# A state-space convolution, two rounds of adapters and a feed-forward layer: moving the convolution's tables, its adds, its input loads and its stores

## The chip, the core and the metric

The kernel runs on one core of a Trainium2 chip. The metric is the device time of one execution, in microseconds (us). The kernel before took 2495.6 us (median of three runs, 2495.14 to 2496.21). The profiled execution took 2497.51 us, of which the span of the core's instructions is 2495.7 us.

## The reference

`x` has 32 sequences of 64 rows of 1024 numbers (`B`, `H`, `L`), float32. Four layers follow each other, each added to `x`:

```python
x = x + conv(x)      # row h is convolved with its own kernel K[h], causal, plus D[h] * x; masked at a length
x = x + x @ w1[id1]  # one 1024 x 1024 matrix for each sequence, picked from 16
x = x + x @ w2[id2]  # the same with other matrices and ids
x = x + down(silu(gate(x)) * up(x))   # 1024 -> 2752 -> 1024, each product with a low-rank term picked by id3
```

The convolution's kernel is a sum over 64 complex exponentials: `K[h, l] = 2 * Re(sum_n Ct[h, n] * exp(dtA[h, n] * l))`. It is computed on the chip as a product of two tables, with `l = 32 a + b`: one table in `a` (tile `gt`), one in `b` (tile `et`), each made of a sine and an exponential, and a small matmul for each row h that sums over n.

## The kernel before, in words

**Layout.** The 32 sequences are four chunks of 8 (`NCK`, `BC`). A chunk of `x` is a tile of 128 partitions by 8 x 512 numbers, 16 KB a partition, 2 MB in all (`x_tile`). Chunks 0 and 1 lie in `xpool` (two buffers). Chunks 2 and 3 lie in `x2pool` only while the convolution runs; then they are stored to DRAM (tiles `xd`, L141, on ScalarE's DMA queue), which frees their space for the feed-forward's pools, and each is loaded back when its chunk is near (`between`, `parked`).

**Convolution** (`convolution`, from L560). First some sixty small VectorE operations on 128 x 64 and 128 x 128 tiles (L617 to L686), from the tables `par` (L576) and `cst` (L105). Then the 64 rows go in four groups of 16 (`HG`). `kernels(g)` makes a group's tables: four products `bth` and `brho` (`powers`), three sines (`sine`, L597 to L605: seven VectorE operations and one ScalarE activation each), five more products, all on 128 x 512 tiles; 16 matmuls into `pk` (L745); a copy to `ks` (L753), an add (line 591 is the helper `tt` of all these products), and a store to DRAM (`kp`, L757 and L758, ScalarE's queue). `convolve(g)` reads the stored kernel back from SP's queue as Toeplitz blocks `hk` of 1 MB for two rows (L770, three buffers) together with `uf`, 0.5 MB for four rows (L765), runs 32 matmuls for each `hk` (L781) into `pc`, multiplies by the mask into `tmp` (two buffers), and for every four rows adds `tmp` to the four chunks of `x` (four adds of 128 x 256). All products and adds are VectorE's. In the program `kernels(g + 1)` stands ahead of `convolve(g)`, so that TensorE, which keeps the program's order, meets the `pk` matmuls of group 1 ahead of the first `pc`. The four loads of `x` (L692) are on ScalarE's queue.

**Adapters** (`adapter`, `adapters`). Chunk c needs, for 8 sequences and 2 layers, 8 weight blocks of 0.5 MB each: 128 loads, 64 MB. They go through `wpool` (nine buffers of 4 KB a partition) on SP's queue (L176), and each pair of blocks feeds four matmuls (L182). A pair of sequences ends with two ScalarE copies to `y` (L192), eight transposes (L200) and two VectorE adds to `x` (L204).

**Feed-forward** (`ffn`). For each of 11 strips of the hidden dimension `gated` loads four weight blocks, combines them on VectorE (`stationary`, L347 to L350), runs seven products for gate and for up (L377), copies and adds the results (`u` L391, `c` L393 and on), and adds the low-rank term `lt` (L329). The down product is in `po` (L505), four parts `h` for each of two blocks. The low-rank columns come from `columns`: eight small loads on ScalarE's queue into `raw`, then a ScalarE copy to `at` (L255). `prepare(c)` makes the low-rank products of gate and up of a chunk (`pl_g`, `pl_u`, L276) and the combinations `xd` of its `x`; for a later chunk it stands in the last part `h` of the chunk before.

**Order.** While chunk c is in its feed-forward, the adapters of chunk c + 1 run between its strips: `other(share)` counts work and takes the next of 17 pieces when it is due. For chunk 0 there is nothing to run beside: its adapters run alone, all of them ahead of its feed-forward. TensorE's order is the program's; the other engines' orders are set by a scheduler at build time. [...]

Of the kernel before, what the change touches and what calls it, by code (L numbers as in the profile page):

```python
# [8 lines left out]
F32 = mybir.dt.float32  # L9
# [18 lines left out]
MB = 6  # L28
SEG = 3
# [6 lines left out]
HG = 16  # L36
# [25 lines left out]
def kernel(  # L62
# [42 lines left out]
    nc.sync.dma_start(cst, consts)  # L105
    ident = cst[:, CO_ID : CO_ID + P]
    bmask = cst[:, CO_BM : CO_BM + 2 * H]

# [22 lines left out]
    def x_tile(pool, c, tag):  # L131
        return pool.tile([P, KT, TC], F32, tag=tag, name=f"x{c}")

    xs = [x_tile(xpool, c, "x") for c in range(2)]
    parked = []
    with tc.tile_pool(name="x2pool", bufs=1) as x2pool:
        late = [x_tile(x2pool, c, f"x{c}") for c in range(2, NCK)]
        convolution(tc, cst, xt, xf, ssm, lens, xs + late, ps_tile)
        for c, x_c in enumerate(late, 2):
            d = dpool.tile([P, KT, TC], F32, tag=f"xd{c}", name=f"xd{c}")  # L140
            nc.scalar.dma_start(d, x_c)  # L141
            parked.append(d)

    loads = []
    ypool = ctx.enter_context(tc.tile_pool(name="ypool", bufs=2))

    def adapter(w, layer, b0, pending):
        c, lo = b0 // BC, (b0 % BC) * H
        es = []
        for b in (b0, b0 + 1):
            with ExitStack() as after:
                if len(loads) > 1:

                    after.enter_context(tc.issue_after(loads[-2]))
                es.append(
                    nc.values_load(  # L160
                        ids_sb[0:1, layer * B + b : layer * B + b + 1],
                        engines=[SP],
                        min_val=0,
                        max_val=NE - 1,
                    )
                )
        acc = [acc_tile(f"pa{layer}_{b0}_{i}") for i in range(2)]
        for kt in range(KT):
            if kt == KH:
                yield  # L170
            if kt == (c == 0) and pending:
                residual(*pending.pop())
            wts = []
            for s, e in enumerate(es):
                wt = wpool.tile([P, L], F32, tag="w", name=f"wa{layer}_{b0 + s}_{kt}")
                load = nc.sync.dma_start(  # L176
                    wt, w[bass.ds(e, 1), kt].rearrange("e p f -> p (e f)")
                )
                wts.append(wt)
            for i in range(2):  # L180
                for s in range(2):
                    nc.tensor.matmul(  # L182
                        acc[i][s * H : (s + 1) * H, :],
                        xs[c][:, kt, lo + s * H : lo + (s + 1) * H],
                        wts[s][:, i * 512 : (i + 1) * 512],
                        start=(kt == 0),
                        stop=(kt == KT - 1),
                    )
        loads.append(load.ins)
        y = ypool.tile([P, L], F32, tag="y", name=f"y{layer}_{b0}")  # L190
        for i in range(2):
            nc.scalar.copy(y[:, i * 512 : (i + 1) * 512], acc[i])  # L192
        pending.append((c, lo, y, f"{layer}_{b0}"))
        yield
# [24 lines left out]
    hpool = ctx.enter_context(tc.tile_pool(name="hpool", bufs=1))  # L219
    gpool = ctx.enter_context(tc.tile_pool(name="gpool", bufs=2))  # L220
    apool = ctx.enter_context(tc.tile_pool(name="apool", bufs=MB))

# [194 lines left out]
    def prepare(c):  # L417

        x_c = xs[c]
        for name, table in (("g", ag), ("u", au)):  # L420
            at = columns(table, c, KT, f"{name}_{c}")
            ps = low_rank(at, KT, lambda i: (x_c[:, i, :], P), f"{name}_{c}")
            nc.vector.tensor_mul(tms[name], ps, bmask)
# [12 lines left out]
    def ffn(c, xb, others):  # L436
# [6 lines left out]
        def other(share, of=2 * FM * AT_GATED + (2 * KH - 2) * AT_DOWN):  # L443
            due[0] += share * (NPIECE + 1)
            while due[1] * of < due[0]:
                next(others, None)
                due[1] += 1
# [8 lines left out]
        for block, (m0, m1) in enumerate(BLOCKS):  # L456
# [26 lines left out]
            for h in range(KH):  # L483
                name = f"{c}_{block}_{h}"
                if last and h == KH - 1 and c + 1 < NCK:
                    for _ in others:
                        pass
                    ready = prepare(c + 1)
# [56 lines left out]
                if not last or h < KH - 2:  # L545
                    other(AT_DOWN)
        return ready

    with tc.manual_schedule(engines={PE}):
        for _ in adapters(0):  # L550
            pass
        xb = prepare(0)
        for c in range(NCK):
            xb = ffn(c, xb, adapters(c + 1) if c + 1 < NCK else iter(()))


def convolution(tc, cst, xt, xf, ssm, lens, xs, ps_tile):
# [9 lines left out]
    with ExitStack() as ctx:  # L567
# [8 lines left out]
        nc.sync.dma_start(par, ssm)  # L576
        ln = s1.tile([P, B], I32, tag="len", name="ln")
        nc.sync.dma_start(ln, lens.partition_broadcast(P))
        aim, cre, cim, dskip = (par[:, i, :] for i in range(2, 6))
# [10 lines left out]
        def tt(o, a, b, op):  # L590
            nc.vector.tensor_tensor(o, a, b, op)
            return o
# [98 lines left out]
        for c in range(NCK):  # L691
            nc.scalar.dma_start(xs[c], xt[:, c])  # L692

# [3 lines left out]
        def kernels(g):  # L697

            h0 = g * HG
            shape = [P, HG, LQ]  # L700

            def over_l(ap):
                return ap[:, h0 : h0 + HG].unsqueeze(2).to_broadcast(shape)

# [5 lines left out]
            def big(tag):  # L710
                n[0] += 1
                return s1.tile(shape, F32, tag=f"b{tag}", name=f"b{tag}{g}_{n[0]}")

            def powers(at, tag):
                theta, rho = big(f"th{tag}"), big(f"rho{tag}")
                tt(theta, over_l(y), over_h(at), ALU.mult)
                tt(rho, over_l(x), over_h(at), ALU.mult)
# [17 lines left out]
            gt = s2.tile(shape, F32, tag="gt", name=f"gt{g}")  # L735
            et = s2.tile(shape, F32, tag="et", name=f"et{g}")
# [7 lines left out]
            for i in range(HG):  # L744
# [7 lines left out]
            ks = s2.tile([LQ, HG, LQ], F32, tag="ks", name=f"ks{g}")  # L752
            nc.vector.tensor_copy(ks.rearrange("a h b -> a (h b)"), ps[:LQ, : HG * LQ])  # L753
            k0 = ks[0:1, :, 0]
            tt(k0, k0, dskip[0:1, h0 : h0 + HG], ALU.add)
            kp = dram.tile([HG, KROW], F32, tag=f"kp{g}", name=f"kp{g}")
            nc.scalar.dma_start(kp[:, :P], zero)  # L757
# [3 lines left out]
        def convolve(g, kp):  # L761
            for h0 in range(0, HG, 4):
                ha = g * HG + h0
                uf = s3.tile([P, 4, KT, B], F32, tag="uf", name=f"uf{ha}")
                nc.sync.dma_start(uf, xf[:, ha : ha + 4])  # L765
                tmp = s2.tile([P, 4, KT * B], F32, tag="tmp", name=f"tmp{ha}")
                for i in range(0, 4, 2):
                    hk = s3.tile([P, 2, L], F32, tag="hk", name=f"hk{ha + i}")

                    nc.sync.dma_start(  # L770
                        hk,
                        bass.AP(
                            tensor=kp.tensor,
                            offset=kp[h0 + i : h0 + i + 1, 1:2].offset,
                            ap=[[1, P], [KROW, 2], [1, L]],
                        ),
                    )
                    ps = ps_tile(f"pc{ha + i}").rearrange("p (i t) -> p i t", i=2)
                    for j in range(2):
                        for d in range(KT):  # L780
                            nc.tensor.matmul(  # L781
                                ps[:, j, d * B :],
                                hk[:, j, d * P : (d + 1) * P],
                                uf[:, i + j, : KT - d, :].rearrange("p k b -> p (k b)"),
                                start=(d == 0),
                                stop=(d == KT - 1),
                            )
                    tt(
                        tmp[:, i : i + 2, :],
                        ps,  # L790
                        maskf.unsqueeze(1).to_broadcast([P, 2, KT * B]),
                        ALU.mult,
                    )
                tv = tmp.rearrange("p i (k b) -> p k b i", b=B)
                for c in range(NCK):
                    xv = xs[c].rearrange("p k (b h) -> p k b h", h=H)[
                        :, :, :, ha : ha + 4
                    ]
                    tt(xv, xv, tv[:, :, c * BC : (c + 1) * BC, :], ALU.add)

        ready = kernels(0)
        for g in range(H // HG):
            nxt = kernels(g + 1) if g + 1 < H // HG else None
            convolve(g, ready)
            ready = nxt

# [132 lines left out]
```

## Time and profile before

| | us |
|---|---|
| median of three runs | 2495.6 |
| profiled execution | 2497.51 |
| its span | 2495.7 |
| TensorE busy in the span | 2397.1 (96%) |
| VectorE busy | 1141.7 (46%) |
| ScalarE busy | 337.7 (14%) |
| GpSimd busy | 50.1 (2%) |
| DMA moved | 500.53 MB, mean 201 GB/s |

A matmul's end is modelled in these records, so a busy TensorE is not one at its peak: while it waits for weights that arrive one by one its matmuls show as long ones. In the lines below "PE" is TensorE's matmuls, "PEld" its weight loads, DVE VectorE, ACT ScalarE, POOL GpSimd, "SPq" and "ACTq" the queues of SP and ScalarE. A group's line gives the source line, the engine, the operation, out<-in, shapes, the count; then busy time, the mean of one in ns, and the idle time just before with what ended it.

### The profile page before, as it was taken

How to read it: one execution, taken by the hardware profiler on the slowest of the kernel's cores; microseconds unless marked ns; L12 is line 12 of the kernel's file. 1: busy time of each engine (PE TensorE's matmuls, PEld its weight loads, DVE VectorE, ACT ScalarE, POOL GpSimd, SP SyncE). 2: the span in 40 equal slices, each digit the busy share in tenths (PEclk: the TensorE clock that was granted, in tenths of full speed). 3: DMA queues.
4: the chain of work that ended last, by engine and by line, in shares of the span. 5: the costliest groups of instructions: out<-in, count | busy, mean ns of one | idle time of the engine just before them, and what ended most of it. 6: DMA issues, size and time to landing. Idle time of an engine off the chain costs nothing.

```text
span 2495.7 us, 34972 instructions
## 1 busy us (share of the span) xinstructions
PE 2397.1 (96%) x13600; PEld 1802.8 (72%) x13600; DVE 1141.7 (46%) x2184; ACT 337.7 (14%) x644; POOL 50.1 (2%) x52
## 2 busy tenths in 40 slices
PE   0998898999999999999999999999999999999999
PEld 0995234777777777768686776777777688888887
DVE  8732002445344553444344453444345445554554
ACT  3100001111011111111011201111011101210110
POOL 0000000000000000000000000000000000000000
PEclk9999999999999999999999999999999999999999
DMA  7787997555655546565656547564746544223221
GB/s 294 245 281 280 378 409 279 220 202 198 211 207 203 211 144 239 202 225 182 222 186 226 191 158 243 193 244 156 246 164 248 182 135 136 85 74 107 89 66 62
DMA packets 176167, 500.53 MB, mean 201 GB/s; under 512 B 19778, under 2 KB 69250, under 8 KB 174978
## 3 DMA queue, kind: packets, MB, share of 16 engines
q1 hardware_dynamic: 145762, 453.43, 51.4%
q10 hardware_dynamic: 26144, 31.24, 3.6%
q0 software_dynamic: 4096, 13.63, 1.6%
q8 instruction: 107, 1.75, 0.3%
q14 instruction: 58, 0.48, 0.1%
HBM read 485.36 MB, written 12.88 MB: 200 GB/s over the span
## 4 chain that ended last, share of the span: by engine, by line
PE 89%; DMA 8%; DVE 2%; ACTq 1%; issue 1%; ACT 0%; SPq 0%; DVEq 0%
PE pf L377 42%; PE po L505 21%; PE pa L182 15%; PE pc L781 6%; DMA wa<-in_w 6%; PE pe L319 2%; PE py L200 1%; PE pl_d L276 1%; PE po L302 1%; DMA x<-xd 1%; DMA out_y<-x 0%; DMA x<-in_xt 0%; PE pl_g L276 0%; ACTq L250 0%; ACTq L244 0%
## 5 line engine op out<-in xcount | busy, mean ns | idle before, releaser
L377 PE MATMUL pf<-xd,wf 128*128 128x256 f32 (+1 forms) x2816 | 668.6, 382 | 0.0
L377 PEld LDWEIGHTS pf<-xd,wf 128*128 128x128 f32 (+1 forms) x2816 | 524.0, 188 | 96.8 <-issue 9.7
L182 PE MATMUL pa<-wa,x 128*64 128x512 f32 x2048 | 495.1, 603 | 26.4 <-DMA wa<-in_w 20.2
L377 PE MATMUL pf<-xd,s 128*128 128x256 f32 (+1 forms) x2112 | 500.9, 380 | 5.0 <-ACT c L393 4.9
L377 PEld LDWEIGHTS pf<-xd,s 128*128 128x128 f32 (+1 forms) x2112 | 397.0, 188 | 65.8 <-ACT c L393 5.3
L182 PEld LDWEIGHTS pa<-wa,x 128*64 128x64 f32 x2048 | 150.1, 137 | 336.1 <-issue 251.9
L505 PE MATMUL po<-act,wd 128*128 128x256 f32 x704 | 177.0, 385 | 0.0
L505 PE MATMUL po<-actd,s 128*128 128x256 f32 x704 | 172.9, 379 | 0.0
L505 PE MATMUL po<-actd,wd 128*128 128x256 f32 x704 | 172.9, 379 | 0.0
L402 DVE TENSOR_TENSOR c<-pf,u 128x256 f32<-128x256 f32 (+1 forms) x88 | 37.3, 424 | 267.8 <-PE pf L377 267.8
L505 PEld LDWEIGHTS po<-act,wd 128*128 128x128 f32 x704 | 130.3, 190 | 33.3 <-issue 11.0
L781 PE MATMUL pc<-uf,hk 128*128 128x256 f32 (+7 forms) x1024 | 149.8, 310 | 0.0
L781 PEld LDWEIGHTS pc<-uf,hk 128*128 128x128 f32 x1024 | 146.0, 193 | 3.6
L505 PEld LDWEIGHTS po<-actd,s 128*128 128x128 f32 x704 | 133.6, 190 | 18.4
L505 PEld LDWEIGHTS po<-actd,wd 128*128 128x128 f32 x704 | 133.6, 190 | 18.4
L329 ACT COPY lt<-pe 128x512 f32<-128x512 f32 (+1 forms) x176 | 90.3, 599 | 260.7 <-PE pe L319 146.8
L347 DVE TENSOR_TENSOR s<-wf 128x512 f32<-128x512 f32 x88 | 60.7, 690 | 131.8 <-PE po L505 50.8
L204 DVE TENSOR_TENSOR x<-py,x 128x512 f32<-128x512 f32 x64 | 42.9, 687 | 153.9 <-PE py L200 153.7
L406 DVE TENSOR_TENSOR c<-c,lt 128x1024 f32<-128x1024 f32 (+1 forms) x88 | 107.5, 1222 | 5.1 <-DVE c L404 0.5
L192 ACT COPY y<-pa 128x512 f32<-128x512 f32 x64 | 37.5, 585 | 467.3 <-PE pa L182 442.8
L347 DVE TENSOR_TENSOR s<-wd 128x384 f32<-128x384 f32 x64 | 33.4, 522 | 138.4 <-PE po L505 79.7
L400 ACT COPY c<-pf 128x256 f32<-128x256 f32 (+1 forms) x88 | 32.7, 372 | 418.9 <-PE pf L377 418.9
(146 smaller groups left out, 1611.5 us busy)
## 6 DMA issues: line engine op xcount, KB each, us to landing
wa<-in_w SPq DMA_DIRECT2D x512, 512.0 KB
wf<-in_wg SPq DMA_DIRECT2D x88, 512.0 KB
wf<-in_wu SPq DMA_DIRECT2D x88, 512.0 KB
wd<-in_wd SPq DMA_DIRECT2D x96, 384.0 KB
hk<-kp SPq DMA_DIRECT2D x32, 1024.0 KB
x<-in_xt ACTq DMA_DIRECT2D x4, 2048.0 KB
uf<-in_xf SPq DMA_DIRECT2D x16, 512.0 KB
wd<-in_wd SPq DMA_DIRECT2D x32, 256.0 KB
```

What stands on the lines that cost most here:

```text
L182: nc.tensor.matmul(acc[i][s * H : (s + 1) * H, :], xs[c][:, kt, lo + s * H : lo + (s + 1) * H], wts[s][:, i * 512 : (i + 1) * 512], start= ...
L192: nc.scalar.copy(y[:, i * 512 : (i + 1) * 512], acc[i])
L204: nc.vector.tensor_add(cols, ps, cols)
L319: nc.tensor.matmul(ps[:n, at_ : at_ + 2 * H], bt[pair(j), g, i, :n], tms["gu"[g]][pair(j)], start=(g + i == 0), stop=True, skip_group_chec ...
L329: nc.scalar.copy(lt[:n, :, 2 * H * j : 2 * H * (j + 1)], ps[:n].rearrange("p (i t) -> p i t", i=4),)
L347: nc.vector.tensor_add(s1, a21, a22)
L377: nc.tensor.matmul(ps, ws[j][:, kt, :n], xb[j][:, kt, :], start=start and kt == 0, stop=kt == KH - 1, skip_group_check=True,)
L400: nc.scalar.copy(cq[:n, 0], pa)
L402: nc.vector.tensor_add(cq[:n, 1], pb, u[:n])
L406: nc.vector.tensor_add(cf, cf, lt[:n, g].rearrange("p i t -> p (i t)"))
L505: nc.tensor.matmul(pss[j], ws[j][:k, i, :], ab[m - m0][j], start=(m == m0 and home[j] % 2 == 0), stop=(m == m1 - 1), skip_group_check=True,)
L781: nc.tensor.matmul(ps[:, j, d * B :], hk[:, j, d * P : (d + 1) * P], uf[:, i + j, : KT - d, :].rearrange("p k b -> p (k b)"), start=(d == ...
```

## The change

Four things are changed in the convolution, and with them where its data lies.

- **Groups.** Five groups of 8, 8, 16, 16 and 16 rows in place of four of 16. `kernels(g + 1)` now stands inside group g, behind its first four rows where g has 8, behind its first eight where it has 16; the first `pc` comes straight behind the first `pk`.
- **Engines.** `bth` and `brho` and the adds to `x` go from VectorE to GpSimd. The copy of `pk` to `ks` goes from VectorE to ScalarE.
- **Loads.** `par`, `cst` and `lens` are the first DMAs on SP's queue, the four chunks of `x` follow on the same queue, then `uf` and `hk`. The ids (`ids`, `il`) come behind the first of the `hk`. The first adapter's first eight weight loads are put behind the sixth `hk`: four of them go to new buffers (`epool`), which with `wpool`'s nine makes thirteen.
- **Chunks 2 and 3.** They and the four new buffers lie on the other side of the SBUF. Their stores (`park`) are issued behind the last ScalarE copy of chunk 0's adapters, no longer at the convolution's end; the pool `apool` takes their place.

Beside these, `prepare` is split: the gate's part stands one part `h` earlier than the up's, the adapters' pieces of the next chunk are due one part earlier, and several pools wait for tiles rather than for the whole of an earlier pool.

```diff
+EARLY = 4
-HG = 16
+GROUPS = (8, 8, 16, 16, 16)
+HG = max(GROUPS)
...
-    nc.sync.dma_start(cst, consts)
...
+    right = ExitStack()
+    x2pool = right.enter_context(tc.tile_pool(name="x2pool", bufs=1, side="right"))
+    epool = right.enter_context(tc.tile_pool(name="epool", bufs=1, side="right"))
+    late = [x_tile(x2pool, c, f"x{c}") for c in range(2, NCK)]
+    early = [epool.tile([P, L], F32, tag=f"e{i}", name=f"early{i}") for i in range(EARLY)]
+    blocks = convolution(tc, cst, consts, xt, xf, ssm, lens, xs + late, ps_tile)
+    parked = []
+
+    def park():
+        for c, x_c in enumerate(late, 2):
+            d = dpool.tile([P, KT, TC], F32, tag=f"xd{c}", name=f"xd{c}")
+            nc.scalar.dma_start(d, x_c)
+            parked.append(d)
...
-    with tc.tile_pool(name="x2pool", bufs=1) as x2pool:
-        late = [x_tile(x2pool, c, f"x{c}") for c in range(2, NCK)]
-        convolution(tc, cst, xt, xf, ssm, lens, xs + late, ps_tile)
-        for c, x_c in enumerate(late, 2):
-            d = dpool.tile([P, KT, TC], F32, tag=f"xd{c}", name=f"xd{c}")
-            nc.scalar.dma_start(d, x_c)
-            parked.append(d)
...
-                wt = wpool.tile([P, L], F32, tag="w", name=f"wa{layer}_{b0 + s}_{kt}")
+                name = f"wa{layer}_{b0 + s}_{kt}"
+                wt = early.pop(0) if early else wpool.tile([P, L], F32, tag="w", name=name)
...
-        def other(share, of=2 * FM * AT_GATED + (2 * KH - 2) * AT_DOWN):
+        def other(share, of=2 * FM * AT_GATED + (2 * KH - 3) * AT_DOWN):
...
-                if last and h == KH - 1 and c + 1 < NCK:
+                if last and h >= KH - 2 and c + 1 < NCK:
                     for _ in others:
                         pass
-                    ready = prepare(c + 1)
+                    ready = prepare(c + 1, "gu"[h - KH + 2])
...
-    with tc.manual_schedule(engines={PE}):
-        for _ in adapters(0):
-            pass
-        xb = prepare(0)
+    with tc.issue_after(blocks[5]):
+
+        pieces = adapters(0)
+        next(pieces)
+    for _ in pieces:
+        pass
+    with tc.issue_after(copies[-1]):
+        park()
+    right.close()
+    apool = ctx.enter_context(
+        tc.tile_pool(name="apool", bufs=MB, side="right", reuse_waits="tile")
+    )
+    prepare(0, "g")
+    xb = prepare(0, "u")
...
         nc.sync.dma_start(par, ssm)
+        nc.sync.dma_start(cst, consts)
         ln = s1.tile([P, B], I32, tag="len", name="ln")
         nc.sync.dma_start(ln, lens.partition_broadcast(P))
+        for c in range(NCK):
+            nc.sync.dma_start(xs[c], xt[:, c])
...
-        for c in range(NCK):
-            nc.scalar.dma_start(xs[c], xt[:, c])
...
-                tt(theta, over_l(y), over_h(at), ALU.mult)
-                tt(rho, over_l(x), over_h(at), ALU.mult)
+                nc.gpsimd.tensor_tensor(theta, over_l(y), over_h(at), ALU.mult)
+                nc.gpsimd.tensor_tensor(rho, over_l(x), over_h(at), ALU.mult)
...
-            nc.vector.tensor_copy(ks.rearrange("a h b -> a (h b)"), ps[:LQ, : HG * LQ])
+            nc.scalar.copy(ks.rearrange("a h b -> a (h b)"), ps[:LQ, : hg * LQ])
...
-                    tt(xv, xv, tv[:, :, c * BC : (c + 1) * BC, :], ALU.add)
+                nc.gpsimd.tensor_tensor(xv, xv, tv[:, :, c * BC : (c + 1) * BC, :], ALU.add)
...
         ready = kernels(0)
-        for g in range(H // HG):
-            nxt = kernels(g + 1) if g + 1 < H // HG else None
-            convolve(g, ready)
+        ha = 0
+        for g, hg in enumerate(GROUPS):
+            nxt = None
+            for row in range(0, hg, 4):
+                convolve(ready, row, ha)
+                ha += 4
+                if row == max(hg - 12, 0) and g + 1 < len(GROUPS):
+                    nxt = kernels(g + 1)
             ready = nxt
+        return loads
```

## The prediction

> **What bounds the kernel now.** I read the busy time by stage first, then TensorE's waits, then the order of time around each wait. The windows are: tables until the first `pc`, the convolution, chunk 0's adapters, the step into the feed-forward, the rest. Columns: length, busy TensorE, its weight loads, VectorE, ScalarE, GpSimd (instructions in brackets), TensorE's clock, DMA share, GB/s.
>
> ```profile
> 0.00:61.18 61.18, 3.76 (x64) 3.56 (x64) 50.48 (x151) 19.19 (x24) 0.20 (x4) 1.00 0.76 300
> 61.18:214.52 153.34, 151.94 (x1091) 148.17 (x1089) 81.17 (x148) 9.36 (x12) 0.00 (x0) 1.00 0.73 245
> 214.52:396.20 181.68, 160.46 (x572) 49.40 (x572) 11.50 (x20) 12.40 (x19) 2.02 (x2) 0.97 0.99 389
> 396.20:424.40 28.20, 21.50 (x222) 17.52 (x222) 10.41 (x16) 6.54 (x10) 1.46 (x1) 0.88 0.49 164
> 424.40:2495.70 2071.30, 2059.45 (x11657) 1584.16 (x11656) 988.16 (x1853) 290.17 (x580) 46.41 (x45) 1.00 0.52 178
> ```
>
> So VectorE sets the first 61 us, TensorE the convolution, DMA the 182 us of the adapters (share 0.99, weight loads only 49 us), TensorE the last 2071 us. The change acts on the first four rows. The waits say the same:
>
> ```profile
> PE pk L745 <- DVE gt L591: 40.1, 1, 40.1
> PE pa L182 <- DMA wa<-in_w: 20.2, 37, 6.6
> PE pk L745 <- DVE et L591: 17.3, 1, 17.3
> PE pf L377 <- ACT c L393: 4.9, 1, 4.9
> PE pl_u L276 <- ACT at_u L255: 4.6, 4, 1.2
> ```
>
> 40.1 us pass until group 0's tables exist, and 17.3 us more go to group 1's, which stand ahead of the first `pc`. The 4.9 us are one stall at 409 to 414 us, which the order of time explains:
>
> ```profile
> 399.97 6.41 ACTq L250 DMA_DIRECT2D raw_d<-in_ad  x8
> 412.18 1.47 ACT L255 COPY at_d<-raw_d 128x1536 f32<-128x1536 f32 x1 [3.70 <-issue]
> 413.56 0.36 ACT L391 COPY u<-pf 128x256 f32<-128x256 f32 x1
> 414.25 3.78 PE L377 MATMUL pf<-xd,s 128*128 128x256 f32 x8 [4.93 <-ACT c L393]
> ```
>
> ScalarE issues eight small loads, waits for them in `at_d`, and only then makes the copies `u` and `c` that free TensorE's banks.
>
> [...] Here ScalarE's store moved 3.83 MB at 217 to 230 us while SP's weights moved 0.67 MB[...].
>
> **The change, part by part**
>
> *First tables.* VectorE begins its first operation on `par` at 10.0 us, since two 2 MB loads of `x` were queued first. With `par` first I take the 64 KB `kp` store's 1.76 us from issue to the load that waits for it (43.86 to 45.62), some more for 192 KB, and start at 3.5 us. From there to the last of group 0's tables VectorE took 30.0 us (10.0 to 40.1). Rows to reprice them:
>
> ```profile
> L591 DVE TENSOR_TENSOR bth<-sm,cst 128x512 f32<-128x512 f32 x8 | 5.5, 682 | 0.0
> L597 DVE TENSOR_SCALAR bk<-bth,cst 128x512 f32<-128x512 f32 x12 | 5.7, 478 | 0.0
> L591 DVE TENSOR_TENSOR x<-x,tmp 128x256 f32<-128x256 f32 x60 | 32.2, 597 | 0.4
> L591 DVE TENSOR_TENSOR tmp<-pc,mask 128x512 f32<-128x512 f32 x31 | 21.4, 690 | 67.5 <-PE pc L781 67.5
> ```
>
> Two-input operations fall from 682 ns at 512 columns to 215 at 64, so 256 fewer columns save 0.27 us on each of 14; the one-input ones (450 to 187) save 0.15 on each of 12: 5.5 us for 8 rows in place of 16. Four table products leave for GpSimd: 2.4 us. Eleven operations of group 1 stand ahead of the last table in the new order, about as much as group 1 had there before. So 30.0 - 7.9 = 22.1, and 3.5 + 22.1 = 25.6 us. GpSimd's products[...] and ScalarE's table loads (1.28 us each) lie between them, so I take 28 (25.6 to 32). From the last table to the first `hk` issue before: 40.1 to 45.6. Now ScalarE's copy and `kp` store are queued behind an exponential and a table load: 7 us. The first `hk` then needs about 5.5 us (the DMA view shows 210 to 260 GB/s for its first 1 MB). First `pc` at 28 + 7 + 5.5 = 40.5 us (36 to 47) against 61.2: -20.7.
>
> *The convolution.* TensorE's 152.0 us stay, plus 1.7: of the small `pk` matmuls 56 rows' worth are now inside in place of 32 (1.13 us for 16). A later group's kernel needs about 9 us from `pk` to a landed `hk`, and one block of four rows, 9.36 us, covers it for groups 1 and 2, two blocks for 3 and 4. VectorE has group 3 and 4's tables to make in the same 30 us[...]. I take 3 us of stall (0 to 10). The last add costs 0.7 (`tmp`) and a GpSimd add instead of 1.4 in all: +0.6. GpSimd's adds: [...]1.0 (0.6 to 2), four per 9.36 us, hidden. At 1.0 us they end with TensorE; the cover fails at 2.34. `ks` on ScalarE (0.67 on VectorE) is in the 7 us. Weights and `x` in this stage are hidden: the DMA share is 0.73 and 10.5 us before its end are idle (25 GB/s at 206 to 216.5). `ids` behind `hk` cost nothing, their users come later. Chunk 0's first `pa`: 40.5 + 152.0 + 1.7 + 3 + 2 = 199.2 against 214.5, -15.3 (-25 to -2).
>
> *Adapters.* 181.7 us from the first `pa` to the last `y` copy. In the middle the DMA runs at 409 GB/s, 1.28 us a block; the 119 blocks not yet loaded are 152 us, the two stores 10.2, the gathers and columns 3. The rest is start, end and a thin stretch at 245 to 257 us (135 to 330 GB/s), some 6 us, right behind the stores. Afterwards 115 blocks: 147.2 us. But the four extra buffers aren't used again; the first of the nine comes free after the third pair, 4.9 us in, where it was about 2. So the four blocks (5.1 us) are worth only some 2. Sum: 4.9 + 1.5 (first landing) + 147.2 + 4 (last landing, matmuls, copy) = 157.6, plus 3 for half of the thin stretch: 160.6, or -21 (-27 to -13).
>
> *The step into the feed-forward.* The stores don't vanish: they are issued on ScalarE's queue right behind the last `y` copy, ahead of `raw_d`. In the built order the fifth `raw_d` load waits for the second store to land[...], the last one for a weight block on SP that itself waits for the first store. Queued behind on ScalarE are `at_d`, the last `lt` copy, `u` and `c`, for which TensorE waits. Before, `u` came 17.4 us after the last `y` copy (396.2 to 413.6). Stores and the weights in flight are 4.2 + 2.5 MB, 16.5 us at 409 GB/s; then the last loads, 2 us of landing, 1.5 us of `at_d`: `u` 23.4 us after. +6 (0 to +12). Nothing else needs the stores soon.
>
> *Split `prepare`.* TensorE waits 1.16 us for `at_u` at each of three later chunks; the gate's part a block earlier removes it: -3 (-3.5 to 0). Earlier due pieces ask 4% more of a DMA at half load: nothing. Pool waits by tile: nothing on the path.
>
> Sum: -15.3 - 21 + 6 - 3 = -33.3. Against the profiled execution that is a span of 2462.4 and 2464.2 in all; the median of the runs lies 1.9 below that execution, so I name 2462.
>
> **The rivals.**
> (A) *The gain at the start is eaten.* GpSimd and VectorE block each other, the early kernels come late (10 us of stall, first `pc` at 45) the thin stretch of the adapters stays, and the step costs 10: 2495.6 - 4 - 18 + 10 - 3 = 2481. For: many waits back and forth between the two engines. Against: VectorE has 81 us of work in 153.
> (B) *All is as summed, and the stores are hidden*: no cost at the step, no stall in the convolution, 2453. For: DMA share 0.49 in that stage. Against: the queue order above.
> (C) *GpSimd becomes the bound: slower.* Its adds start at about 55 us behind the table products. 64 adds of c us end at 55 + 64c. The other terms save 18, so it breaks even where the first `pa` is at 232.5: c = 2.8 us. At 3.5 us it is at 280: 2495.6 + 65.5 - 18 = 2543. For: [...]VectorE itself takes 597 ns where 256 columns should take about 420.[...]
> (D) *The DMA bounds from the start, so nothing moves.* Until 396 us it moves about 118 MB; at 409 GB/s, and 340 for `hk`, that is 315 us. The forecast puts the adapters' end at 360, above that floor. Time: 2495.
>
> **How the numbers follow.** Forecast (2455 to 2470) 0.55; B and better 0.15; A 0.20; C 0.05; D 0.05. Range: 2445 to 2482, which takes in A's price and B with the lower bounds. It leaves out C, D and the worst of A. A measurement of this kernel tells about 0.2% (5 us) from no change. Faster: forecast, B, A, 0.91. Same: D, 0.04. Slower: C, 0.05.
>
> **What would show it.** First `pc` at 36 to 47 us; convolution 155 to 165 us long; GpSimd adds under 2.3 us; adapters 155 to 168 us long with the DMA share near 1; `u` later after the last `y` copy than 17.4 us, with a TensorE stall of about 11; no `pl_u` wait at later chunks. A GpSimd add over 2.3 us, or a first `pc` after 55 us, would make it wrong.

## The result and the profile after

The changed kernel took 2478.0 us (median of four runs, 2475.95 to 2481.69) against 2495.4 us of the kernel before beside it: a ratio of 0.9934, with a 95% interval of 0.9917 to 0.9951. It is faster by 17.4 us; 33 were forecast. The time lies inside the stated range (2445 to 2482), close to the 2481 of rival A. The profiled execution took 2475.95 us, its span 2474.2 us, and it is the quickest of the four; the sums below are made against the two spans, which differ by 21.5 us.

First the windows, cut at the same events as before: first `pc`, first `pa`, last `y` copy of chunk 0, first `pa` of chunk 1. Columns: length, busy TensorE, weight loads, VectorE, ScalarE, GpSimd, TensorE's clock, DMA share, GB/s.

```profile
0.00:41.69 41.69, 1.07 (x17) 0.96 (x17) 37.06 (x133) 15.75 (x24) 12.63 (x16) 1.00 0.71 271
41.69:210.62 168.93, 158.05 (x1136) 153.66 (x1137) 73.27 (x111) 18.74 (x24) 65.10 (x70) 0.97 0.79 273
210.62:373.27 162.65, 153.42 (x572) 48.80 (x572) 9.71 (x16) 12.43 (x19) 4.44 (x5) 1.00 1.01 399
373.27:407.43 34.16, 22.14 (x220) 17.62 (x221) 10.43 (x16) 6.45 (x10) 0.95 (x1) 0.85 0.69 263
407.43:2474.20 2066.77, 2058.84 (x11657) 1582.96 (x11656) 986.05 (x1853) 291.16 (x580) 47.67 (x45) 1.00 0.52 179
```

The lengths to set beside the earlier ones: 61.18 became 41.69, 153.34 became 168.93, 181.68 became 162.65, 28.20 became 34.16, and 2071.30 became 2066.77. So -19.5, +15.6, -19.0, +6.0 and -4.5. The forecast had -20.7, +5.4, -21, +6 and -3. Four of the five are close to it; the second, the convolution, is 10.2 us off.

TensorE's waits say where in the convolution the time went:

```profile
PE pk L766 <- DVE bet L614: 28.7, 1, 28.7
PE pc L804 <- DMA hk<-kp: 11.9, 1, 11.9
PE pf L386 <- ACT lt L338: 8.9, 1, 8.9
PE pa L191 <- DMA wa<-in_w: 8.5, 34, 1.0
PE pc L804 <- DVE bre L624: 6.1, 1, 6.1
PE pc L804 <- issue: 3.1, 1, 3.1
PE pl_u L285 <- ACT at_u L264: 1.1, 1, 1.1
```

The first two are the way to the first `pc` (28.7 in place of 40.1; the 17.3 us for `et` are gone). `pl_u` waits once, not four times. The 6.1 and 3.1 us are new. The order of time at the group changes shows them, TensorE's rows and those of the chain from `pk` to `hk`:

```profile
53.38 0.69 PE L766 MATMUL pk<-bet,bgt 128*32 128x32 f32 x16
54.00 9.39 PE L804 MATMUL pc<-uf,hk 128*128 128x256 f32 x64
58.57 0.32 ACTq L779 DMA_DIRECT2D kp<-ks  x1
66.49 11.01 PE L804 MATMUL pc<-uf,hk 128*128 128x256 f32 x64 [3.10 <-issue]
77.43 1.20 PE L766 MATMUL pk<-bet,bgt 128*32 128x32 f32 x32
78.56 9.39 PE L804 MATMUL pc<-uf,hk 128*128 128x256 f32 x64
84.27 0.56 ACT L774 COPY ks<-pk 32x512 f32<-32x512 f32 x1
86.11 0.31 ACTq L779 DMA_DIRECT2D kp<-ks  x1
87.89 1.41 SPq L792 DMA_DIRECT2D hk<-kp  x3
94.03 20.41 PE L804 MATMUL pc<-uf,hk 128*128 128x256 f32 x128 [6.09 <-DVE bre L624]
```

A block of four rows takes 9.39 us when its `hk` are there. From `pk` to the first `pc` of the new group pass 13.1 us (53.38 to 66.49) and 16.6 us (77.43 to 94.03). Group 2's chain: `ks` copied 5.7 us after the `pk` end, stored at 86.1, its `hk` issued at 87.9, used at 94.0. From the store (`kp`) to that first `pc` pass 7.9 us in both; the two differ in what passes from `pk` to the store, 5.2 and 8.7 us. The wait is written down to `bre` of VectorE, which has no part in it: `pc` needs `hk`, and `hk` was issued 6.1 us earlier, about what such a load takes (the first one: 35.4 to 41.7). The blocks of 11.76, 11.01 and 20.41 us (two of 9.36) are long in their first row: its 16 matmuls take 4.47, 3.87 and 4.15 us, a later row's 2.30. The second `hk` is not late in the first and the last of them: it landed at 44.1 and 96.5 us, its first matmuls start at 48.7 and 100.5. In the last two the trace shows a granted clock of 0.50 (67.1 to 70.5 and 91.0 to 97.8 us); for the first it has no record of a lower clock, and what slows that row is not shown.

The step into the feed-forward, where the stores now stand:

```profile
372.74 0.82 ACTq L129 DMA_DIRECT2D xd<-x  x2
377.06 17.65 ACTq L259 DMA_DIRECT2D raw_d<-in_ad  x8
395.39 3.78 PE L386 MATMUL pf<-xd,wf 128*128 128x256 f32 x8 [8.90 <-ACT lt L338]
396.54 1.47 ACT L264 COPY at_d<-raw_d 128x1536 f32<-128x1536 f32 x1 [0.23 <-DMA raw_d<-in_ad]
398.40 0.38 ACT L400 COPY u<-pf 128x256 f32<-128x256 f32 x1
```

The eight `raw_d` issues took 6.41 us before and take 17.65 behind the two stores. `u` comes 25.1 us after the last `y` copy (17.4 before), and TensorE's longest stall here has grown from 4.9 to 8.9 us.

GpSimd's new work, by shape (busy time, mean of one in ns), and one of VectorE's rows in the first 100 us:

```profile
L820 POOL TENSOR_TENSOR x<-x,tmp 128x256 f32<-128x256 f32 x64 | 56.4, 915 | 86.5 <-DVE tmp L614 86.5
L738 POOL TENSOR_TENSOR bth<-sm,cst 128x512 f32<-128x512 f32 x6 | 8.7, 1450 | 15.3 <-DVE bre L622 9.9 <-DVE brq L622 5.4
L738 POOL TENSOR_TENSOR bth<-sm,cst 128x256 f32<-128x256 f32 x4 | 3.6, 911 | 10.5 <-DVE sm L614 7.2 <-DVE bre L622 3.4
```

```profile
L620 DVE TENSOR_SCALAR bk<-bth,cst 128x512 f32<-128x512 f32 x9 | 7.8, 872 | 0.0
```

The adds take 915 ns, far from the 2.8 us at which rival C would have begun. But the same `bk` row was 478 ns before: this operation of VectorE's is slower where GpSimd works too.

### The profile page after: what moved, and what is told of

Same layout as the page of the kernel before. It is cut to its first block, busy times and chain, and to the rows that moved or that the text cites. A ratio compares the mean times of both kernels' runs of the same rounds, so it can differ in the third digit from the quotient of the medians.

```text
span 2474.2 us, 35037 instructions
## 1 busy us (share of the span) xinstructions
PE 2393.5 (97%) x13600; PEld 1804.0 (73%) x13600; DVE 1116.5 (45%) x2127; ACT 344.5 (14%) x656; POOL 130.8 (5%) x136
## 4 chain that ended last, share of the span: by engine, by line
PE 88%; DMA 8%; DVE 4%; issue 0%; ACTq 0%; SPq 0%; POOL 0%; ACT 0%; DVEq 0%
PE pf L386 42%; PE po L515 22%; PE pa L191 14%; DMA wa<-in_w 5%; PE pc L804 5%; PE pe L328 2%; PE py L210 1%; PE pl_d L285 1%; DMA xd<-x 1%; PE po L311 1%; DMA x<-xd 1%; DMA out_y<-x 0%; DVE bk L620 0%; DVE bsp L614 0%; DMA wf<-in_wu 0%; PE pl_u L285 0%
## 5 line engine op out<-in xcount | busy, mean ns | idle before, releaser
L191 PE MATMUL pa<-wa,x 128*64 128x512 f32 x2032 | 482.9, 598 | 12.4 <-DMA wa<-in_w 8.5
L515 PE MATMUL po<-actd,wd 128*128 128x256 f32 x704 | 172.9, 379 | 0.0
L515 PEld LDWEIGHTS po<-actd,wd 128*128 128x128 f32 x704 | 133.6, 190 | 18.4
L234 POOL DMA_INDIRECT bgu<-in_bgu,rows x44 | 46.9, 1066 | 1809.3 <-PE pe L328 1690.8
```

What stands on the lines that cost most here:

```text
L191: nc.tensor.matmul(acc[i][s * H : (s + 1) * H, :], xs[c][:, kt, lo + s * H : lo + (s + 1) * H], wts[s][:, i * 512 : (i + 1) * 512], start= ...
L234: nc.gpsimd.indirect_dma_start(out=t, out_offset=None, in_=table, in_offset=bass.IndirectOffsetOnAxis(ap=rows[:, c, piece : piece + 1], axis=0
L515: nc.tensor.matmul(pss[j], ws[j][:k, i, :], ab[m - m0][j], start=(m == m0 and home[j] % 2 == 0), stop=(m == m1 - 1), skip_group_check=True,)
```

## The experiments

My theory after this result: the lost 10 us of the convolution come from *where `pk` stands*. `kernels(g + 1)` is emitted behind the first four rows of a group of 8, so that one block of four rows, 9.4 us of TensorE's work, has to cover a chain (`pk`, copy, add, store, load of `hk`) of 13 to 17 us. I call this short cover. The rivals: GpSimd slows VectorE, so that the tables and the add to `ks` come late; or the `ks` copy waits in ScalarE's queue.

The stall in a run is read as the convolution's length over 155.7 us: 152.0 of TensorE before, 1.7 for `pk` inside it, 2 at its end (the forecast's terms without a stall). By that the changed kernel has 13.2 us. What the slow first rows behind a wait cost is part of it. It comes on top of what the kernel before loses in its own first row (4.38 us, the next 2.30): there the first four blocks took 39.05 us and the next four 36.98. The runs of one kernel lie up to 9 us apart, so totals under some 4 us apart are not told from each other. The stages come from one profiled execution of each kernel. How far they repeat is seen from the changed kernel and the three below whose edits touch only the stores or the first weights: the convolution takes 168.6 to 170.0 us in these four, and the first `pc` stands at 41.3 to 44.4.

**The engines: adds, products, both.**

```diff
-                nc.gpsimd.tensor_tensor(xv, xv, tv[:, :, c * BC : (c + 1) * BC, :], ALU.add)
+                nc.vector.tensor_tensor(xv, xv, tv[:, :, c * BC : (c + 1) * BC, :], ALU.add)
```

> The adds to x go back to VectorE, the table products stay on GpSimd. Changed kernel: first pc 41.7 us, first pa 210.6, some 14 us of stall between them. Theory (short cover: from pk to a landed hk takes 13 to 17 us and one block of four rows covers 9.4): the stalls stay within 3 us, first pa 209 to 216, total 2476 to 2484. Rival (GpSimd slows VectorE[...], so tables and the add to ks come late): VectorE's one-input operations fall from 872 toward 480 ns behind the first tables, the stalls shrink by 5 us or more, first pa 205 or earlier, total about 2472.

Measured: first `pc` 41.8, first `pa` 208.1, convolution 166.3 us, so a stall of 10.6. Total 2475.0 us, ratio 0.9932 (0.9918 to 0.9946), as the changed kernel. `bk` fell only to 649 ns, since the table products were still on GpSimd. The stall is within 3 us of 13.2, as short cover says; the first `pa` and the total lie 1 us below the ranges that I gave for it, and short of the rival's.

```diff
-                nc.gpsimd.tensor_tensor(theta, over_l(y), over_h(at), ALU.mult)
-                nc.gpsimd.tensor_tensor(rho, over_l(x), over_h(at), ALU.mult)
+                nc.vector.tensor_tensor(theta, over_l(y), over_h(at), ALU.mult)
+                nc.vector.tensor_tensor(rho, over_l(x), over_h(at), ALU.mult)
```

> The products bth and brho go back to VectorE, the adds stay on GpSimd. Short cover: first pc within 2 us of 41.7, stalls within 3 us of 14, total 2475 to 2483. [...]rival: the one-input operations ahead of the first pc fall from 872 to about 480 ns, first pc at 38 or earlier and stalls under 9 us, total about 2469.

Measured: first `pc` at 35.2 us, 6.5 earlier; convolution 166.9, a stall of 11.2. Total 2467.25 us, ratio 0.9894 (0.9879 to 0.9909), which does not overlap the changed kernel's interval. Each theory was half right: the stall stays, as short cover says, but moving the products to GpSimd cost 6.5 us ahead of the first `pc`, where I had expected no more than 2. Group 0's tables are ready at 25.1 us in place of 28.7, and from there to the first `pc` pass 10.1 us in place of 13.0.

With both back on VectorE:

> Both go back to VectorE, GpSimd does nothing in the convolution. Short cover: VectorE's rows are as fast as before (690 and 480 ns) but the stalls are still 10 us or more, since the chain from pk to hk holds no GpSimd work; total 2474 to 2484. [...]rival: stalls under 5 us, first pa about 200, total about 2467. A third reading, that VectorE lacks the time for both, would give 20 us of stall and a total of 2484.

Measured: first `pc` 35.4, convolution 166.4 (stall 10.7), total 2467.0 us, ratio 0.9893 (0.9878 to 0.9909). The total is the one that the rival named, but by the earlier first `pc`; its stall of under 5 us didn't come. VectorE's rows are what they were in the kernel before:

```profile
L738 DVE TENSOR_TENSOR bth<-sm,cst 128x512 f32<-128x512 f32 x6 | 4.1, 681 | 0.0
L620 DVE TENSOR_SCALAR bk<-bth,cst 128x512 f32<-128x512 f32 x8 | 3.8, 477 | 0.0
```

```profile
46.59 0.69 PE L766 MATMUL pk<-bet,bgt 128*32 128x32 f32 x16
58.97 11.01 PE L804 MATMUL pc<-uf,hk 128*128 128x256 f32 x64 [2.37 <-issue]
69.91 1.20 PE L766 MATMUL pk<-bet,bgt 128*32 128x32 f32 x32
84.46 21.48 PE L804 MATMUL pc<-uf,hk 128*128 128x256 f32 x128 [4.04 <-DVE brho L739]
```

So the slowing by GpSimd is real (872 against 477 ns), and it makes at most 2.5 us of the 13.2: with no GpSimd work at all the chain from `pk` to `pc` still takes 12.4 and 14.6 us. In the changed kernel a `bk` that begins at 45.47 us, with GpSimd idle, takes 0.47 us; one that begins at 51.52, during a `brho` of GpSimd's (51.34 to 52.50), takes 1.27 and ends 0.28 us behind it. That VectorE waits for GpSimd's operation there fits these times; by what mechanism is not shown. GpSimd's products themselves are slower than VectorE's were: `bth` takes 1450 against 681 ns at 512 columns and 911 against 414 at 256, 2.1 and 2.2 times, with VectorE at work beside them; GpSimd alone was not measured.

**ScalarE's queue.**

```diff
-            nc.scalar.copy(ks.rearrange("a h b -> a (h b)"), ps[:LQ, : hg * LQ])
+            nc.vector.tensor_copy(ks.rearrange("a h b -> a (h b)"), ps[:LQ, : hg * LQ])
```

> The copy of pk to ks goes back to VectorE; pk, groups and GpSimd's work stay as in the changed kernel. In the changed kernel ks of group 2 waited 5.7 us on ScalarE behind an exponential, a table load and a sine. Theory (one block does not cover the chain on any engine): stalls fall by no more than 4 us, first pa 206 to 212, total 2473 to 2480. Rival (ScalarE's queue is the cause): the chain falls to about 9 us, stalls under 6, first pa 202 or earlier, total 2470 or less.

Measured: the chains got longer, 15.0 and 18.4 us (50.15 to 65.18 and 76.62 to 95.02), the convolution 172.9 us (stall 17.2); first `pc` 39.5, first `pa` 212.3, just above the range that I gave for my theory; total 2477.6 us, ratio 0.9937 (0.9923 to 0.9951). That the copy went to ScalarE is not the cause of the stall: VectorE's queue is no shorter. At group 0 alone the copy on VectorE is worth 2.2 us (first `pc` 39.5 in place of 41.7).

**Larger groups.**

```diff
-GROUPS = (8, 8, 16, 16, 16)
+GROUPS = (16, 16, 16, 16)
```

> Four groups of 16 rows, with pk of the next group behind eight rows, so that two blocks (18.7 us) cover the chain; GpSimd's work as in the changed kernel. Short cover: first pc 8 to 11 us later (50 to 53), but stalls of 4 us or less: first pa 206 to 211, total 2472 to 2479. [...]rival: stalls of 10 us or more stay, first pa 215 to 220, total 2482 to 2488.

Measured: first `pc` at 50.4 us, convolution 157.3 us (stall 1.6), first `pa` 207.7, total 2473.8 us, ratio 0.9929 (0.9915 to 0.9942), all in the ranges for short cover. GpSimd does as much here as in the changed kernel, and two blocks of cover leave no stall to speak of. The eight-row groups bring 8.7 us at the start and lose 11.6 behind it.

**`pk` one block earlier**, nothing else changed:

```diff
-                convolve(ready, row, ha)
-                ha += 4
                 if row == max(hg - 12, 0) and g + 1 < len(GROUPS):
                     nxt = kernels(g + 1)
+                convolve(ready, row, ha)
+                ha += 4
```

> kernels(g + 1) is put one block of four rows earlier in the program than in the changed kernel; GpSimd's work and the groups stay. In the changed kernel group 1's tables exist at 38.0 us and group 2's at 57.4, but TensorE reaches their pk only at 53.4 and 77.4. Theory (the cover is too short because pk stands a block too late): with 18.7 us of cover against a chain of 13 to 17 us the waits at the group changes (3.1 and 6.1 us, and the long blocks behind them) go, first pa at 197 to 201 in place of 210.6, total 2464 to 2471. Rival (GpSimd's slowing of VectorE or ScalarE's queue makes the kernels late, wherever pk stands): 8 us or more of stall stay, first pa 205 or later, total 2473 or more.

Measured: convolution 155.7 us, no stall by the measure above; first `pa` at 197.4; total 2465.1 us, ratio 0.9880 (0.9865 to 0.9896). TensorE's order of time in this kernel:

```profile
38.08 1.06 PE L766 MATMUL pk<-bet,bgt 128*32 128x32 f32 x16 [8.30 <-DVE bgt L614]
41.76 20.42 PE L804 MATMUL pc<-uf,hk 128*128 128x256 f32 x128 [2.61 <-DMA hk<-kp]
62.10 1.20 PE L766 MATMUL pk<-bet,bgt 128*32 128x32 f32 x32
63.23 18.59 PE L804 MATMUL pc<-uf,hk 128*128 128x256 f32 x128
82.70 9.36 PE L804 MATMUL pc<-uf,hk 128*128 128x256 f32 x64 [0.89 <-DMA hk<-kp]
```

Group 1's `pk` now runs while TensorE would only wait for the first `hk`, and the first `pc` comes no later (41.76). The 3.1 us of waiting at the first group change are gone, and 0.9 is left of the 6.1. The first two blocks, 20.42 us, are 1.8 longer than the next two, about what the changed kernel loses in a first row behind a wait (1.6 to 2.2). The chain itself got no shorter: group 2's took 20.6 us here (62.10 to 82.70), with the copy to `ks` again 5.7 us and the store 10.3 us behind the `pk` start, so that two blocks of cover are only just enough. This settles the cause: the same engines, the same groups, the same GpSimd work, and with `pk` earlier all but a few us of the stall are gone.

**Both: earlier `pk`, all on VectorE.** Group 1's `pk` stands in the middle of the first block (`mid`), because the first `pc` is earlier than its tables; the three lines on GpSimd are changed as above.

```diff
+                if i == 0 and mid:
+                    made = mid()
...
-                convolve(ready, row, ha)
+                later = row == max(hg - 12, 0) and g + 1 < len(GROUPS)
+                if later and g:
+                    nxt = kernels(g + 1)
+                mid = (lambda: kernels(1)) if later and not g else None
+                made = convolve(ready, row, ha, mid)
+                nxt = made or nxt
                 ha += 4
-                if row == max(hg - 12, 0) and g + 1 < len(GROUPS):
-                    nxt = kernels(g + 1)
```

> As the last, with all products and adds on VectorE, and group 1's pk in the middle of the first block. Theory: the two gains add up, since the tables on VectorE move the first pc (35.4 us) and the earlier pk removes the stalls: first pa 190 to 194, total 2458 to 2463. Rival: VectorE, with 64 adds and 20 products more, is late with the tables of groups 2 and 3: stalls of 6 us or more, total about 2467 as without the earlier pk. Second rival: the DMA sets the end of chunk 0's adapters, which stays at 366 or later though the first pa comes earlier; total 2465 to 2467.

Measured: first `pc` 35.8, convolution 155.6, first `pa` 191.5, total 2460.55 us, ratio 0.9862 (0.9847 to 0.9877). The two gains add at the first `pa`, and VectorE has time for all of it. The adapters take 166.2 us in place of 162.7 (more on this below) but end at 357.7, so the second rival falls too.

**The stores.** First they go behind the eight `raw_d` loads, and the opening of `apool`, which takes their tiles' place, goes with them; then, in another kernel, back to the convolution's end.

```diff
-    with tc.issue_after(copies[-1]):
-        park()
...
             at = columns(ad[:, block, :, : 2 * nm], c, 2 * nm, f"d{block}_{c}")
+            if not apools:
+                with tc.issue_after(cols[-1]):
+                    park()
```

> The two stores of x are issued behind the first eight raw_d loads of the feed-forward instead of ahead of them. Theory (the 6 us lost at the step come from raw_d waiting behind the stores): from the last y copy to the first u 17 to 20 us in place of 25.7, from there to the first pa of chunk 1 28 to 30 in place of 34, total 2471 to 2474. Rival (the stores' 4.2 MB take the same time from the feed-forward's weights wherever they stand, or the activations wait for the space): the stall moves to a weight or to act, the step stays at 33 or more, total 2476 to 2480.

Measured: from the last `y` copy to `u` 19.8 us, to the first `pa` of chunk 1 30.4 in place of 34.2; total 2472.2 us, ratio 0.9922 (0.9908 to 0.9937), an interval that overlaps the changed kernel's. In this kernel's order of time:

```profile
377.95 6.98 ACTq L259 DMA_DIRECT2D raw_d<-in_ad  x8
385.03 0.39 ACTq L129 DMA_DIRECT2D xd<-x  x1
390.73 0.34 ACTq L129 DMA_DIRECT2D xd<-x  x1
394.00 0.41 ACT L400 COPY u<-pf 128x256 f32<-128x256 f32 x1
```

The issues take 6.98 us again, and `u` comes 5.3 us earlier. In the other kernels that have the stores ahead of `raw_d` the step takes 32.1 to 34.2 us, so the queue order accounts for some 2 to 4 of the step's 6 us.

```diff
+    park()
     ids_sb = cpool.tile([1, 3 * B], I32, tag="ids", name="ids_sb")
...
-    with tc.issue_after(copies[-1]):
-        park()
```

> The two stores of x are issued at the convolution's end, as in the kernel before. Theory (the late stores shorten the adapters by what the DMA needs for them, 10 us and the thin stretch behind them, and cost 6 at the step): step back at 28 us, adapters 170 to 176 us in place of 162.7, total 2478 to 2484. Rival (the adapters are bound by their weights' start and end, the stores were hidden in part): adapters 163 to 166, total 2471 to 2474.

Measured: adapters 176.5 us, 13.8 longer; step 26.0; total 2483.0 us, ratio 0.9954 (0.9940 to 0.9967). The first `pc` came at 44.4, 2.7 us later than in the changed kernel, because VectorE waited 3.41 us for the lengths `ln` in place of 0.67. Kernels with the late stores take 162.7 to 166.8 us for the adapters and 32.1 to 34.2 for the step, so storing late is worth 10 to 14 us in the adapters and costs 6 to 8 at the step; in all 5 us by the medians.

**The first weights.**

```diff
-EARLY = 4
+EARLY = 0
```

> No extra buffers for the first weights, so nine blocks instead of thirteen are loaded ahead of the first pa. Theory (they are used once, worth about 2 us): adapters 164 to 167 us in place of 162.7, total 2478 to 2482. Rival (each block loaded ahead saves its 1.28 us): adapters 167 to 169, total 2482 to 2485.

Measured: adapters 166.8 us, total 2479.75 us, ratio 0.9950 (0.9935 to 0.9964). That looks like 4 us for the four buffers, but the adapters of kernels that have them, with the stores late, lie between 162.7 and 166.8 us too, so it doesn't tell 2 us from 5. Inconclusive.

**The loads of x.**

```diff
-            nc.sync.dma_start(xs[c], xt[:, c])
+            nc.scalar.dma_start(xs[c], xt[:, c])
```

> The four loads of x go back to the head of ScalarE's queue; par stays the first load on SP's. Theory (the two queues' loads share the DMA engines, and par behind x cost VectorE's start 6.5 us): VectorE's first operation on par at 8 to 12 us in place of 3.5, first pc 46 to 50 in place of 41.7, first pa 5 to 8 us later, total 2481 to 2486. Rival (only the smaller groups and the new engines moved the first pc, x is hidden): first pc within 2 us of 41.7, total 2475 to 2481.

Measured: first `pc` at 56.4 us, first `pa` 231.5, total 2497.8 us, ratio 1.0011 (1.0004 to 1.0018): this one line takes back the whole gain, some three times what I expected. Two things that I hadn't priced show in the order of time, VectorE's wait for the lengths `ln`, and ScalarE itself:

```profile
0.75 15.60 ACTq L601 DMA_DIRECT2D x<-in_xt  x4
7.38 0.23 DVE L640 TENSOR_SCALAR exk<-par 128x128 f32<-128x128 f32 x1 [6.39 <-DMA par<-in_ssm]
16.02 0.18 DVE L706 CAST lnf<-ln 128x32 f32<-128x32 int32 x1 [6.93 <-DMA ln<-in_lens]
16.38 1.28 ACT L665 ACT_TABLE_LOAD   x1 [16.38 <-DMA ln<-in_lens]
```

ScalarE spends 15.6 us issuing four 2 MB loads, and its first table load comes at 16.4 us, where the changed kernel has it at 3.7. The group change at 88 us stalls longer too (9.6 us). How much each of these costs was not taken apart.

**All that helped, together:** earlier `pk`, VectorE alone, stores behind `raw_d`.

> The earlier pk, all products and adds on VectorE, and the two stores behind the first raw_d loads, together. If the three edits act at separate places, as measured one by one (first pa 191.5 us, step 30.4 in place of 33.2), the total is 2460.5 - 3 = 2456 to 2459. Rival (the step is set by the DMA, which now has the same bytes in front of it): no gain over 2460.5, 2459 to 2463.

Measured: 2456.5 us (2453.70 to 2460.86), ratio 0.9859 (0.9843 to 0.9875), the lowest median of all these kernels; its interval overlaps that of the kernel with the earlier `pk` and VectorE alone, but its step is 29.2 us where that one has 33.2, as the edit was to do.

## Why the prediction was partly wrong

- *First tables, first `pc` at 40.5: the number right (41.7), in part by luck.* The tables were ready at 28.7 (28 forecast), and 13.0 us passed from there (12.5). What I did not see is that the part given to GpSimd was a loss here: I credited 2.4 us for the products leaving VectorE, and by the runs it cost 6.5 at the first `pc`, 3.6 of them up to the tables. Against that my prices for the tables were too high. With the products on VectorE it takes 22.0 us from its first operation on `par` to the last table (3.1 to 25.1); my sum without the credit gives 24.5. The errors nearly cancelled.
- *The convolution: this step failed.* "A later group's kernel needs about 9 us from `pk` to a landed `hk`, and one block of four rows, 9.36 us, covers it for groups 1 and 2"; "I take 3 us of stall (0 to 10)". Measured 13.1 and 16.6 us, and 13.2 us of stall. The rest of that sum held: without the 3 us it says 155.7, and the kernel with the earlier `pk` takes 155.7 (with one group's `pk`, some 0.6 us, less inside it). For group 0 I had worked out 12.5 us for the same way, and for the later groups I put 9 without a sum. From the `kp` store to the first `pc` pass 7.9 us at groups 0, 1 and 2 of the changed kernel, so 9 us left 1.1 from `pk` to the store (at group 0: stored at 33.8, used at 41.7). That took 5.2, 5.2 and 8.7 us: the copy and the add stand behind operations for the next tables. (This I read from the order of time; no run removed those operations alone.) Even the shortest way in any run, group 0's with the products on VectorE, took 10.1 us, more than one block. No later chain that TensorE waited for took under 12 us in any run here, whichever engine did the copy.
- *GpSimd's adds: right.* 0.9 us (1.0 forecast, my estimate: the trace of the kernel before shows no such operation of GpSimd's), hidden: back on VectorE they change the total by nothing that can be told. Rival C is out.
- *Rival A* (10 us of stall, first `pc` at 45, 2481 us) came nearest in the total, and half of its reason holds. GpSimd and VectorE do hold each other up (`bk` 872 against 477 ns; of GpSimd's `brho` of 512 columns one took 2.70 us, at 36.80 with VectorE's operations beside it, and one 1.16, at 51.34): with the products back on VectorE the first `pc` comes 6.5 us earlier and the total falls by 11 us, to 2467. But the stall, which A put down to this, is for the most part there without GpSimd (10.7 of 13.2 us). Nor did A's thin stretch of the DMA stay: the 30 us that begin 20 us behind the first `pa` ran at 407 GB/s, before at 320.
- *Adapters: near.* 162.7 us against 160.6. My sum left out the 3 us for gathers and columns that I had listed for the kernel before. The late stores were priced at 13.2 us (10.2, and 3 for the thin stretch); by the run that undoes them they are worth 10 to 14.
- *Step: right.* +6.0 against +6, with the mechanism named: `raw_d` behind the stores on ScalarE's queue, some 2 to 4 of the 6 us being that order. `u` itself came 7.7 us later, and my sum for it was not complete: the terms with a price, 16.5 + 2 + 1.5, give 20.0 us, not 23.4, and 25.1 were measured.
- *Split `prepare`: right.* `pl_u` waits only at chunk 0, 1.1 us (4.6 in all before). The last stretch is 4.5 us shorter, where I gave 3 and at most 3.5; the rest of it I can't name.
- *Rival D* (the DMA as a floor at 315 us for the adapters' end) plays no part: the best kernel ends them at 357. Its sum is not right either: 118 MB at D's own rates take 305 us, and the 126.7 MB that the kernel before had moved by then 326.
- *Slips without weight.* The end of the convolution was put at +0.6 us where its own terms (0.7 + 1.0 in place of 1.4) give 0.3, and the chances for faster add up to 0.90, not 0.91.

In the sum: -33.3 forecast, -21.5 in the profiled executions. Of the 11.8 us between them 10.2 are the convolution, 1.2 the first `pc`, 2.0 the adapters, less 1.5 won in the last stretch (each rounded). The rest, from 21.5 down to 17.4 by the medians, is the choice of executions: before's profiled one lies 2.1 us above its median, this one 2.1 below.

One thing stays open: with the late stores the adapters take between 162.7 and 166.8 us, and no edit explains which. With the earlier `pk` alone they take 166.8; their first 20 us move 298 GB/s in place of 329, and later both run at 409. An earlier first `pa` is not the reason: the kernel with `x` on ScalarE's queue has its first `pa` at 231.5 us, and its adapters take 166.3. Nor is the gain of the earlier `pk` lost by it: the medians differ by 13 us, as the first `pa` does.

## What to carry to other kernels

When work is cut into smaller pieces to start sooner, price the whole chain that brings the next piece, with the queue ahead of each of its steps, and set it against the cover of one piece; then put the head of the chain where its inputs are ready, not where the loop happens to reach it. Here the inputs of `pk` lay ready for 15 and 20 us (38.0 and 57.4, against 53.4 and 77.4) while TensorE went on with a block that it was about to run out of. And keep large loads off the queue of an engine that has work of its own to do: here four of them on ScalarE's queue cost 20 us.

## What was not expected of the hardware

- ScalarE's instruction stream stood still for 15.6 us while it issued four 2 MB loads; before, two of them took 8.57. On SP's queue the issue of the same four took 2.97 us in the changed kernel; why they differ is not shown.
- A one-input VectorE operation of 512 columns (`bk` from `bth`) took 477 ns with GpSimd idle in the convolution and 872 on average with GpSimd's products and adds beside it.
- A wait's named releaser can be an engine without any part in it: `bre`, `brho` and "issue" stand where the trace's times point to `hk`.
